# Last layer, second half of the batch: tile order by column pairs, and six of eight pairs turned by VectorE instead of TensorE

## The chip, the cores and the metric

The kernel runs on one core of a Trainium2 chip. The metric is the device time of one execution in microseconds; of the kernel before, three runs were timed, and the median is what is compared.

## What is computed

The reference takes x of shape (1024, 16, 16, 16): 1024 images of 16 rows (h), 16 columns (w) and 16 channels (c), float32. Four layers follow, each `x = x + layer(group_norm(x))`:

- layer 0, a tensor-train matrix on the 4096 values of an image;
- layer 1, a "cellular automaton" update: two fixed 3x3 depthwise filters, a dense layer 48 to 128 with relu, a dense layer 128 to 16, and a mask (alive or not, from a 3x3 maximum);
- layer 2, a 3x3 convolution;
- layer 3, the same kind of update as layer 1 with its own weights.

```
h = relu(flat @ fc0_w.T + fc0_b)
d = (h @ fc1_w.T + fc1_b).reshape(B, C, W, Hh)
xn = (xt + d) * (pre & post)
```

The result goes out in the layout of the input: batch, h, w, c.

## The kernel before, in words

**Tiling.** The batch is cut into two chunks of 512 images. Inside the layers the 512 images are the columns of a tile and 128 values of an image are its partitions; a chunk is 32 such tiles of 128x512 float32 (256 KB each). In layer 3 a tile is named by (q, w2): four channels (4q to 4q+3), two neighbouring columns (2·w2 and 2·w2+1, the "column pair" w2) and all 16 rows. The result wants images on partitions, so every tile of layer 3 has to be turned (transposed).

**The last stage.** The change is in the last stage, layer 3 on the second chunk, `layer_nca(X1, 1, 3, L3, xo)`, which takes the end of the span. Its work is driven by an order written out by `plan()`: a list of slots. A slot is either one matmul on each of up to four row groups of TensorE (tile `ph`, line L1466) or the second dense layer of one column of a tile (`fc1`, tile `po`, L1317). The result of a `ph` row is taken by ScalarE (relu into `hid`, L1469). A tile (q, w2) has two columns v = 0, 1, one "quad" m each, so there are 64 quads. Step by step:

- When a quad m begins, SyncE's DMA queue (SP) gets the load of the weights `wq` of quad m+2 (L1275, only for q > 0, five buffers), and, for the few columns that need them, four small copies `nx` (L1291) for a later quad: FAR quads ahead.
- At `fc1` of v = 0 SP gets the load of the residual tile `r` (L1298, four buffers).
- At `fc1` of v = 1 VectorE (DVE) makes `u` from `po` (L1329), which also frees the PSUM bank of `po` (two banks in all, shared with the turning); GpSimd (POOL) multiplies by the mask and adds to `r` (L1368, L1369). For q = 0 the masks come first (L1361, L1362).
- Eight slots later `turn` (L1378) transposes the four 128x128 blocks of `r` on TensorE into a PSUM bank `ptx`, and DVE copies it out (`evac`, L159, two copies per tile) into `xo`, which lies in the 8 MB of X0, free by then.

**Beside it.** The same stage brings the first chunk's result out: `output_steps(0)`, sixteen rounds h = 0..15. Each loads 512 KB of the finished first chunk from DRAM in four DMAs of 128 KB (`xs`, L963), turns it by four DVE block transposes (`xo`, L969) and stores 512 KB to the result (L974). `run()` spreads these steps over the stage: a step has a cost, its position is the sum of the costs ahead of it, and a step of cost 0 stands at the position reached so far, just ahead of the next step that has a cost. A `turn` of a round costs 1, its load and store cost 0. Two buffers `xs` and two `xo` are there, and the load of round h+1 is put ahead of the turn of round h.

**Queues.** Each engine works through its instructions in the order in which the program gives them, SP too: where an SP entry waits (for a buffer to be free, for data to be finished), the SP entries behind it wait with it. In the last stage SP's own waits show 79.8 us in 30 waits of a `wq` load (L1275) for TensorE.

**After the stage** eight DMAs of 1 MB (L1606) write the second chunk's result from X0.

Of the kernel before, what the change touches and what calls it, by code (L numbers as in the profile page):

```python
# [18 lines left out]
B, S, C = 1024, 16, 16  # L19
P = 128  # L20
NB = 512
# [82 lines left out]
def conv_preact_kernel(ctx: ExitStack, tc: tile.TileContext, a: dict, out: bass.AP):  # L104
    nc = tc.nc
    V, A, G, T = nc.vector, nc.scalar, nc.gpsimd, nc.tensor
# [9 lines left out]
    xf = [  # L116
        [dram.tile([8, 4, P, NB], F32, tag=f"xf{l}_{n}", name=f"xf{l}_{n}") for n in range(NCH)]
        for l in range(5)
    ]
# [7 lines left out]
    def stage(es, sb, ps):  # L127

        for key, sizes, kw in (("sb", sb, {}), ("ps", ps, {"space": PSUM})):
            p = es.enter_context(  # L130
                tc.tile_pool(name=f"{key}{len(pool)}", bufs=1, reuse_waits="tile", **kw)
            )
            pool[key] = p, sizes
        pool[len(pool)] = None

    def work(shape, tag, name, dt=F32):
        p, sizes = pool["sb"]
        return p.tile(shape, dt, tag=tag, name=name, bufs=sizes[tag])
# [10 lines left out]
    def psum(shape, name):  # L149
        return bank(shape, shared[0], name)  # L150
# [3 lines left out]
    def evac(dst, src):  # L154
        flip[0] ^= 1
        if flip[0] and not on_vector[0]:
            A.copy(dst, src)
        else:
            V.tensor_copy(dst, src)  # L159


    ident = const.tile([P, P], F32, tag="ident", name="ident")
# [504 lines left out]
    def rstd(st, rows=slice(0, P)):  # L667


        def root():  # L670
            st["t"] = work([P, NB], "s", "t")
            A.activation(st["t"][rows], st["ve"][rows], AF.Sqrt)

        def newton():
            ve, t = st["ve"][rows], st["t"][rows]
            st["r"] = work([P, NB], "n", "r")
            r = st["r"][rows]
            V.reciprocal(r, t)
            V.tensor_tensor(t, r, r, ALU.mult)
            V.tensor_tensor(t, t, ve, ALU.mult)  # L680
            V.tensor_scalar(t, t, -0.5, 1.5, ALU.mult, ALU.add)
            V.tensor_tensor(r, r, t, ALU.mult)

        return [2, root, 3, (6, newton)]
# [64 lines left out]
    def alone(N, q):  # L749

        return (
            N["sums"][q] + [3, N["mean"][q], 1, N["held"][q], 1] + N["sq"][q]
            + [3, N["var"][q], 1, N["keep"][q]]
        )
# [18 lines left out]
    def scaled(N, qs):  # L773
        steps = [N["spread"][qs[0]], 2, N["held"][qs[0]], 2]
        for q in qs:
            mul = N["mul"][q]
            if q < qs[-1]:
                mul = woven(mul, (2, N["spread"][q + 1]), (3, N["held"][q + 1]))
            steps += mul
        return steps  # L780
# [18 lines left out]
    def tile_cw(t, i):  # L799

        return t[i % 8, i // 8]
# [150 lines left out]
    def output_steps(n):  # L952

        steps = []

        lines = xf[4][n].rearrange("w q (c v h) b -> h (q c v) w b", v=2, h=S)

        def load(h, st):  # L960
            st["x"] = work([P, 8, P], "xs", "xs")
            for g in range(4):
                nc.sync.dma_start(st["x"][32 * g : 32 * g + 32], lines[h][:, :, P * g : P * g + P])  # L963

        def turn(h, st):
            st["o"] = work([P, 4, S, S], "xo", "xo")
            x = st["x"].rearrange("p w (j f) -> p f w j", f=4)
            for f in range(4):
                V.transpose(  # L969
                    st["o"][:, f].rearrange("p (w v) c -> p w c v", v=2), x[:, f]  # L970
                )

        def store(h, st):
            nc.sync.dma_start(  # L974
                out[n * NB : n * NB + NB, h].rearrange("(p f) w c -> p f (w c)", f=4),
                st["o"].rearrange("p f w c -> p f (w c)"),
            )

        sts = [{} for _ in range(S)]
        steps += [lambda: load(0, sts[0]), 4]  # L980
        for h in range(S):
            if h + 1 < S:
                steps.append((0, lambda h=h: load(h + 1, sts[h + 1])))
            steps += [lambda h=h: turn(h, sts[h]), (0, lambda h=h: store(h, sts[h]))]
        return steps


# [268 lines left out]
    def layer_nca(X, n, l, L, xo=None):  # L1256


        st = {}
        quads = [(q, w2, v) for q in range(4) for w2 in range(8) for v in range(2)]  # L1260
        AHEAD, FAR = 2, 3
        BANKS, SKEW = 6, (0, 1, 2, 1)

        def rows_of(q, w2, v):
# [99 lines left out]
        def residual(q, w2):  # L1364
            u, r = st["u", q, w2], st["r", q, w2]

            by = V if (q, w2) == (3, 7) else G
            by.tensor_tensor(u, u, st["m"][:, w2], ALU.mult)  # L1368
            by.tensor_tensor(r, r, u, ALU.add)  # L1369
            if xo is None:  # L1370
                after(7, lambda: nc.sync.dma_start(tile_cw(xf[l + 1][n], 8 * q + w2), r))
            else:
                after(8, lambda: turn(q, w2, r))

        def turn(q, w2, r):
            pt = psum([P, 4, 4, 2, S], "ptx")
            for bg in range(4):
                T.transpose(  # L1378
                    pt[:, bg].rearrange("p c v h -> p (c v h)"), r[:, bg * P : bg * P + P], ident
                )  # L1380
            for v in range(2):

                evac(
                    xo[:, :, :, 2 * w2 + v, 4 * q : 4 * q + 4].rearrange("p g h c -> p g c h"),
                    pt[:, :, :, v],
                )
# [7 lines left out]
        def after(n, fn):  # L1394
            later.append((st["slot"] + n, fn))
# [83 lines left out]
    def run(layer, us, loads, *spans, by=0.0):  # L1479

        start, main = layer
        start()
        loads, done = list(loads), 0
        todo = []
        for bg, lo, hi in spans:
            bg = [b if isinstance(b, tuple) else (1, b) if callable(b) else (b, None) for b in bg]
            idle = sum(b[0] for b in bg if b[1] is None) / (us * (hi - lo))  # L1490
            less = min(1.0, 0.7 / idle) if idle else 1.0
            weight = sum(b[0] for b in bg if b[1] is not None)
            at = lo
            for cost, step in bg:
                if step is None:
                    at += cost * less / us
                else:
                    todo.append((at, step))
                    at += (hi - lo) * (1 - idle * less) * cost / weight
        todo.sort(key=lambda x: x[0])  # L1500
        for i, step in enumerate(main):
            step()
            part = (i + 1) / len(main)
            while done < len(loads) and done < len(loads) * part / (by or 1e-9):
                loads[done]()
                done += 1
            while todo and (todo[0][0] < part or i == len(main) - 1):
                todo.pop(0)[1]()
# [4 lines left out]
    X0, X1 = XN  # L1513
# [18 lines left out]
    with ExitStack() as es:  # L1532
# [30 lines left out]
        for q in range(4):  # L1563
            bg = alone(N, q - 1) if q else [0.0]
            if q == 3:
                bg = bg + rstd(nst, slice(0, 96)) + [3] + scaled(N, range(3))
# [6 lines left out]
    nca_sb = dict(t4=2, s=3, n=2, wq=5, mask=1, f=5, hid=8, u=2, r=4, nx=1)  # L1573
    nca_ps = dict(h=6, o=2)
    conv_sb, conv_ps = dict(gn, s=3, r=12, hx=3), dict(o=6, m=2)
    on_vector[0] = True
    with ExitStack() as es:
        shared[0] = "o"
        stage(es, nca_sb, nca_ps)
        run(  # L1580
            layer_nca(X0, 0, 1, L1), 250, load_cw(X1, xf[1][1]), (last, 0.0, 0.18),
            (norm_cw(X1, False), 0.21, 1.0), by=0.3,
        )
        run(
            layer_nca(X1, 1, 1, L1), 245, load_wc(X0, xf[2][0]), (norm_lines(X0, False), 0.2, 1.0), by=0.3
        )
# [7 lines left out]
    with ExitStack() as es:  # L1594
        shared[0] = "o"
        stage(es, nca_sb, nca_ps)
        run(layer_nca(X0, 0, 3, L3), 245, load_cw(X1, xf[3][1]), (norm_cw(X1, False), 0.2, 1.0), by=0.3)
    with ExitStack() as es:
        stage(es, dict(nca_sb, xs=2, xo=2), nca_ps)

        xo = X0.rearrange("p n b -> p (n b)").rearrange("p (g h w c) -> p g h w c", g=4, h=S, w=S)
        run(layer_nca(X1, 1, 3, L3, xo), 280, (), (output_steps(0), 0.0, 1.0))
        for h in range(0, S, 8):
            for g in range(4):
                b0 = NB + g * P
                nc.sync.dma_start(  # L1606
                    out[b0 : b0 + P, h : h + 8].rearrange("b h w c -> b (h w c)"),
                    xo[:, g, h : h + 8].rearrange("p h w c -> p (h w c)"),
                )


# [25 lines left out]
```

## Time and profile before

| what | us |
|---|---|
| median of three runs (3052.56 to 3057.89) | 3057.21 |
| the profiled execution | 3054.15 |
| its span, first to last instruction | 3052.4 |
| last stage, first to last work on TensorE | about 2763 to 3030 |
| writing the second chunk's result out at the end | 3030 to 3052.4 |

In the profile PE is TensorE, PEld its weight loads, DVE VectorE, ACT ScalarE, POOL GpSimd, SP SyncE with its DMA queue. Lines such as L1378 are lines of the kernel before. A row of a group of instructions gives the line, engine, operation, output and input, how many, then busy time and the mean of one in ns, then idle time ahead of them and what ended it. The chain of waits follows the work that ended last backwards; the timeline gives start and duration of each instruction.

### The profile page before, as it was taken

Reading aid. Unit: us, or ns where it says so; the run is one execution under the profiler, and the core shown is the slowest. Engines: PE = TensorE matmul, PEld = TensorE weight load, DVE = VectorE, ACT = ScalarE, POOL = GpSimd, SP = SyncE. Lnnn points to the kernel's source line nnn. Section 1 sums busy time; section 2 is a strip of 40 time slices with the busy share of each in tenths; the row PEclk is TensorE's granted clock in tenths of the full one; section 3 lists DMA queues with packets and bytes.
Section 4 is the critical chain, followed back from the end, with each engine's and each line's share of the span. In section 5 each row is a group of like instructions: output and inputs, shape, how many; then the busy total and the mean of one; then the engine's idle time right before and its main releaser. Section 6 shows DMA issues by size and latency. Waiting matters only on the chain.

```text
span 3052.4 us, 36639 instructions
## 1 busy us (share of the span) xinstructions
PE 2982.6 (98%) x13746; PEld 1252.2 (41%) x13746; DVE 1757.4 (58%) x2338; ACT 1100.0 (36%) x1798; POOL 674.8 (22%) x732
## 2 busy tenths in 40 slices
PE   7999999999999999999999999999999999999996
PEld 5544334444444444444444433333333333333332
DVE  5254336555554555544555768756977766856432
ACT  4431341100000000000111156666667656666563
POOL 1114671200000000000000015434542223442331
PEclk8999999999999999999999999999999999999998
DMA  7642664533333433332222235436337866343555
GB/s 260 257 146 88 137 140 156 179 107 116 109 110 126 151 109 109 109 102 88 88 88 94 71 123 172 132 123 202 123 125 177 193 101 204 123 129 112 149 163 197
DMA packets 251809, 418.67 MB, mean 137 GB/s; under 512 B 35044, under 2 KB 105320, under 8 KB 248560
## 3 DMA queue, kind: packets, MB, share of 16 engines
q1 hardware_dynamic: 225376, 362.45, 35.9%
q0 software_dynamic: 25440, 53.58, 8.5%
q8 instruction: 109, 1.79, 0.2%
q14 instruction: 68, 0.56, 0.1%
q10 hardware_dynamic: 816, 0.30, 0.0%
HBM read 238.79 MB, written 165.60 MB: 132 GB/s over the span
## 4 chain that ended last, share of the span: by engine, by line
issue 47%; PE 43%; POOL 5%; DMA 1%; DVE 1%; ACT 0%; SPq 0%; POOLq 0%; DVEq 0%
PE ph L1466 17%; PE po L1098 13%; PE po L1317 6%; PE po L1193 2%; POOL u L1368 2%; POOL res L1369 2%; PE pw L1021 1%; PE L_conv_pe L392 1%; PE ptin L840 1%; POOL xf L1242 1%; PE ptx L1378 1%; DMA gq<-g_dram 0%; PE pr L739 0%; PE pvar L727 0%; PE pmean L723 0%
## 5 line engine op out<-in xcount | busy, mean ns | idle before, releaser
L1098 PE MATMUL po<-xn,w 128*128 128x512 f32 x3584 | 1577.4, 597 | 4.6 <-DVE xn L911 4.6
L1098 PEld LDWEIGHTS po<-xn,w 128*128 128x128 f32 x3584 | 672.3, 191 | 841.5 <-issue 818.3
L1469 ACT ACTIVATE hid<-ph,pack 128x512 f32<-128x512 f32 x1024 | 652.5, 686 | 380.5 <-PE ph L1466 271.0
L1134 DVE TENSOR_TENSOR r<-r,po 128x512 f32<-128x512 f32 x576 | 378.1, 684 | 577.0 <-PE po L1098 525.9
L1368 POOL TENSOR_TENSOR u<-u,mask 128x512 f32<-128x512 f32 x124 | 195.8, 1579 | 1817.4 <-DMA nx<-xn 1239.7
L1026 ACT COPY w<-pw 128x512 f32<-128x512 f32 (+1 forms) x320 | 150.6, 557 | 1214.4 <-issue 1014.5
L1466 PE MATMUL ph<-xn,wq 32*128 32x512 f32 x3664 | 565.7, 610 | 0.0
L1466 PEld LDWEIGHTS ph<-xn,wq 32*128 32x128 f32 x3664 | 232.8, 184 | 270.2 <-issue 238.2
L1466 PE MATMUL ph<-xn,pack 32*128 32x512 f32 x1288 | 297.5, 623 | 1.2 <-DVE mask L1362 0.9
L1317 PE MATMUL po<-hid,pack 128*32 128x512 f32 x2048 | 282.5, 606 | 2.7 <-ACT hid L1469 2.7
L1039 DVE TENSOR_TENSOR w<-w 128x512 f32<-128x512 f32 x320 | 210.5, 685 | 99.8 <-ACT w L1026 99.8
L640 DVE TENSOR_TENSOR xn<-xn,m 128x1024 f32<-128x1024 f32 x160 | 225.5, 1458 | 47.1 <-ACT m L655 47.0
L1329 DVE SCALAR_TENSOR_TENSOR u<-po,pack,xn 128x512 f32<-128x512 f32 x128 | 95.9, 749 | 204.7 <-PE po L1317 200.3
L1369 POOL TENSOR_TENSOR res<-res,u 128x512 f32<-128x512 f32 x124 | 207.5, 1673 | 9.7
L1193 PE MATMUL po<-xn,convw 128*128 128x512 f32 x368 | 166.8, 606 | 5.1 <-ACT conv L1241 5.1
L1466 PEld LDWEIGHTS ph<-xn,pack 32*128 32x128 f32 x1288 | 115.8, 185 | 98.4 <-issue 62.7
L1134 DVE TENSOR_TENSOR xn<-xn,po 128x512 f32<-128x512 f32 x96 | 64.4, 685 | 125.9 <-PE po L1098 125.8
L1317 PEld LDWEIGHTS po<-hid,pack 128*32 128x32 f32 x2048 | 43.1, 109 | 197.4 <-issue 137.7
L607 DVE TENSOR_TENSOR sq<-sq 128x1024 f32<-128x1024 f32 x78 | 106.9, 1370 | 13.1 <-ACT sq L625 10.8
L1193 PEld LDWEIGHTS po<-xn,convw 128*128 128x128 f32 x368 | 69.2, 193 | 102.1 <-issue 92.0
L404 POOL DMA_DIRECT2D L_conv_wy<-xn x160 | 88.8, 563 | 28.5 <-ACT xn L398 17.6
L1021 PE MATMUL pw<-R,gq 32*128 32x256 f32 (+1 forms) x1280 | 88.9, 383 | 2.3 <-DMA gq<-g_dram 2.3
(165 smaller groups left out, 1775.2 us busy)
## 6 DMA issues: line engine op xcount, KB each, us to landing
xf<-r SPq DMA_DIRECT2D x112, 512.0 KB, 3.9
xn<-xf SPq DMA_DIRECT2D x96, 512.0 KB, 5.0
r<-xf SPq DMA_DIRECT2D x80, 512.0 KB, 4.4
wq<-L_conv_wy SPq DMA_DIRECT2D x192, 192.0 KB, 2.7
res<-xf SPq DMA_DIRECT2D x128, 256.0 KB, 3.0
xf<-res SPq DMA_DIRECT2D x96, 256.0 KB, 2.0
res<-xr SPq DMA_DIRECT2D x256, 64.0 KB, 2.8
xf<-conv POOLq DMA_DIRECT2D x64, 256.0 KB, 6.0
```

Of the source, the lines that this page charges most:

```text
L640: V.tensor_tensor(part, part, m().unsqueeze(1).broadcast_to([P, 2, NB]), op)
L1021: T.matmul(pw[r][:, v], st["g", u][rows, v], st["R"][rows, p % 2, 64 * k0 : 256], start=True, stop=True,)
L1026: A.copy(w[:, k0:4, :, 32 * r : 32 * r + 32].rearrange("p k t (v o) -> p v (k t) o", v=2), pw[r],)
L1039: V.tensor_tensor(w[:, k], w[:, x], w[:, y], ALU.add if sign > 0 else ALU.subtract)
L1098: T.matmul(po, st["w", u][:, matrix, t], x, start=t == 0, stop=t == 3)
L1134: V.tensor_tensor(r[at], r[at], po, ALU.add if sign > 0 else ALU.subtract)
L1193: T.matmul(st["po", h][wh], conv["fw"][:, y], X[:, 16 * wh + h + y - 1], start=y == max(0, 1 - h), stop=y == min(2, S - h),)
L1317: T.matmul(po[32 * j : 32 * j + 32], nca["w1"][:, v], hid[j], start=v == 0, stop=v == 1)
L1368: by.tensor_tensor(u, u, st["m"][:, w2], ALU.mult)
L1369: by.tensor_tensor(r, r, u, ALU.add)
L1466: T.matmul(ph, w, x, start=k == 0, stop=k == len(tiles) - 1)
L1469: A.activation(h, ph, AF.Relu, bias=nca["bt"][:, r : r + 1])
```

## The change

In the last stage only:

1. The tiles of q = 1, 2, 3 are taken pair by pair (w2 outer, q inner) instead of q by q. The eight tiles of q = 0 stay first.
2. For the pairs w2 = 0 to 5 no tile is turned on TensorE. Each finished tile is stored to DRAM as in the other layers (seven slots after its residual step). When the tile of q = 3 of a pair is done, the pair is loaded back in two halves k = 0, 1 (`bring`, four DMAs of 128 KB each, 16 and 26 slots later) into the one buffer `xt`, and each half is turned by four DVE block transposes (`turn_blocks`, 25 and 35 slots later). Pairs 6 and 7 are turned on TensorE as before.
3. To make room there is one buffer `xs` and one `xo` instead of two each, and so the load of round h+1 of the first chunk's output comes after the turn and store of round h in the list of steps, not ahead of the turn of round h. `nx` has two buffers instead of one, and its copies are issued two quads ahead instead of three.
4. Images lie on partitions in another order in `xo` (image 4p+f on partition p, part f), so the last eight DMAs write rows of 8 KB that are four images apart.

```diff
@@ output_steps
         for h in range(S):
+            steps += [lambda h=h: turn(h, sts[h]), (0, lambda h=h: store(h, sts[h]))]
             if h + 1 < S:
                 steps.append((0, lambda h=h: load(h + 1, sts[h + 1])))
-            steps += [lambda h=h: turn(h, sts[h]), (0, lambda h=h: store(h, sts[h]))]
@@ layer_nca
-        quads = [(q, w2, v) for q in range(4) for w2 in range(8) for v in range(2)]
-        AHEAD, FAR = 2, 3
+        tiles_in_order = [(q, w2) for q in range(4) for w2 in range(8)]
+        if xo is not None:
+            tiles_in_order = tiles_in_order[:8] + [(q, w2) for w2 in range(8) for q in (1, 2, 3)]
+        quads = [(q, w2, v) for q, w2 in tiles_in_order for v in range(2)]
+        AHEAD, FAR = 2, 3 if xo is None else 2
+        BLOCKS = 6
...
-            if xo is None:
-                after(7, lambda: nc.sync.dma_start(tile_cw(xf[l + 1][n], 8 * q + w2), r))
-            else:
+            if xo is not None and w2 >= BLOCKS:
                 after(8, lambda: turn(q, w2, r))
+                return
+            after(7, lambda: nc.sync.dma_start(tile_cw(xf[l + 1][n], 8 * q + w2), r))
+            if xo is not None and q == 3:
+                for k in range(2):
+                    after(16 + 10 * k, lambda k=k: bring(w2, k))
+                    after(25 + 10 * k, lambda k=k: turn_blocks(w2, k))
+
+        def bring(w2, k):
+            x = st["xs", w2, k] = work([P, 8, P], "xt", "xt")
+            src = xf[l + 1][n][w2].rearrange("q (c v h) b -> (q c v) h b", v=2, h=S)
+            for g in range(4):
+                nc.sync.dma_start(
+                    x[32 * g : 32 * g + 32], src[:, 8 * k : 8 * k + 8, P * g : P * g + P]
+                )
+
+        def turn_blocks(w2, k):
+            x = st["xs", w2, k].rearrange("p h (j f) -> p f h j", f=4)
+            for f in range(4):
+                V.transpose(
+                    xo[:, f, 8 * k : 8 * k + 8, 2 * w2 : 2 * w2 + 2].rearrange("p h v c -> p h c v"),
+                    x[:, f],
+                )
@@ the stage
-        stage(es, dict(nca_sb, xs=2, xo=2), nca_ps)
+        stage(es, dict(nca_sb, nx=2, xs=1, xt=1, xo=1), nca_ps)
```

More of the change, by code (lines that the diff above doesn't have):

```diff
@@ L1369, in residual @@
             by.tensor_tensor(r, r, u, ALU.add)
-            if xo is None:
-                after(7, lambda: nc.sync.dma_start(tile_cw(xf[l + 1][n], 8 * q + w2), r))
-            else:
+            if xo is not None and w2 >= BLOCKS:
                 after(8, lambda: turn(q, w2, r))
+                return
[18 more added lines that the diff above has]
+                )
         def turn(q, w2, r):
             pt = psum([P, 4, 4, 2, S], "ptx")
-            for bg in range(4):
+            for f in range(4):
                 T.transpose(
-                    pt[:, bg].rearrange("p c v h -> p (c v h)"), r[:, bg * P : bg * P + P], ident
+                    pt[:, f].rearrange("p c v h -> p (c v h)"),
+                    r.rearrange("p (j f) -> p f j", f=4)[:, f], ident,
                 )
@@ L1598, in conv_preact_kernel @@
     with ExitStack() as es:
-        stage(es, dict(nca_sb, xs=2, xo=2), nca_ps)
-        xo = X0.rearrange("p n b -> p (n b)").rearrange("p (g h w c) -> p g h w c", g=4, h=S, w=S)
+        stage(es, dict(nca_sb, nx=2, xs=1, xt=1, xo=1), nca_ps)
+        xo = X0.rearrange("p n b -> p (n b)").rearrange("p (f h w c) -> p f h w c", f=4, h=S, w=S)
         run(layer_nca(X1, 1, 3, L3, xo), 280, (), (output_steps(0), 0.0, 1.0))
         for h in range(0, S, 8):
-            for g in range(4):
-                b0 = NB + g * P
+            for f in range(4):
                 nc.sync.dma_start(
-                    out[b0 : b0 + P, h : h + 8].rearrange("b h w c -> b (h w c)"),
-                    xo[:, g, h : h + 8].rearrange("p h w c -> p (h w c)"),
+                    out[NB : 2 * NB, h : h + 8].rearrange("(p f) h w c -> f p (h w c)", f=4)[f],
+                    xo[:, f, h : h + 8].rearrange("p h w c -> p (h w c)"),
                 )
```

## The prediction, made before the changed kernel ran

> **What bounds the kernel now.** First the page's head, to see which engine fills the span.
>
> ```profile
> span 3052.4 us, 36639 instructions
> PE 2982.6 (98%) x13746; PEld 1252.2 (41%) x13746; DVE 1757.4 (58%) x2338; ACT 1100.0 (36%) x1798; POOL 674.8 (22%) x732
> ```
>
> TensorE does. The change lies in the last stage alone, so second the table of windows for it (us, then busy time of PE, PEld, DVE, ACT, POOL, clock, DMA share, GB/s).
>
> ```profile
> 2763.00:3030.00 267.00, 262.54 (x2009) 100.22 (x2008) 115.73 (x199) 163.88 (x256) 75.42 (x62) 1.00 0.51 142
> 3030.00:3052.40 22.40, 0.00 (x0) 0.00 (x0) 0.06 (x1) 0.00 (x0) 0.00 (x0) 0.50 0.90 375
> ```
>
> TensorE is busy 262.5 of 267 us; DVE 43%, POOL 28%, DMA half. Then 22.4 us of output, which wait for the last turning. Third, the groups of the stage, shapes apart, for what is removed and added.
>
> ```profile
> L969 DVE STREAM_TRANSPOSE xo<-xs 128x256 f32<-128x256 f32 x64 | 36.6, 660 | 0.0
> L159 DVE COPY xn<-ptx 128x256 f32<-128x256 f32 x64 | 33.4, 603 | 33.4 <-PE ptx L1378 33.4
> L1378 PE MATMUL ptx<-ident,res 128*128 128x128 f32 x128 | 20.9, 286 | 3.1 <-DVE res L1369 1.9 <-DVE xn L159 1.2
> ```
>
> DVE never sits idle ahead of L969 (0.0): the output rounds of the first chunk find their data there. Fourth, the chain of waits, for what one turning is worth in TensorE's time.
>
> ```profile
> 2995.04 0.59 PE ptx L1378 x4
> 2995.63 2.79 PE ph L1466 x24
> 2998.41 1.00 PE po L1317 x8
> ```
>
> One turned tile: 0.59 us. 24 records of ph are three slots, 0.93 us each; an fc1 slot is 1.00. Fifth, SP's timeline, because the change reorders and adds DMAs, and DVE's beside it for the turns.
>
> ```profile
> 2862.01 0.60 SPq L974 DMA_DIRECT2D out_dram<-xo  x1
> 2862.66 3.08 SPq L963 DMA_DIRECT2D xs<-xf  x4
> 2865.84 4.74 SPq L1275 DMA_DIRECT2D wq<-L_conv_wy  x2
> ...
> 2876.35 0.55 SPq L974 DMA_DIRECT2D out_dram<-xo  x1
> 2876.95 3.02 SPq L963 DMA_DIRECT2D xs<-xf  x4
> ```
>
> ```profile
> 2866.16 2.30 DVE L969 STREAM_TRANSPOSE xo<-xs 128x256 f32<-128x256 f32 x4
> 2883.26 2.26 DVE L969 STREAM_TRANSPOSE xo<-xs 128x256 f32<-128x256 f32 x4
> ```
>
> ```profile
> xs<-xf SPq DMA_DIRECT2D x44, 128.0 KB, 4.5
> ```
>
> The load issued at 2862.66 is turned at 2883.26: it has a whole round (17 us) of lead. But SP passes that place only 4.2 us ahead of DVE's next turn (2862.01 against 2866.16). Over the nine rounds from 2862 to 2988 this distance is 4.2, 6.9, 8.8, -0.4, 0.8, 4.0, 7.7, 1.2 and -7.1 us, 2.9 in the mean.
>
> [...] L1378 needs the copies of L159 behind it, L969 none. [...] copies, u and turns of DVE follow program order. [...] a load of stored data has to wait for the store's completion; SP's waits show one such, 1.6 us, L963 for xf<-res. [...] The trace shows 0.50 only in the idle tail, no gap inside a stage.
>
> **The change, part by part.**
>
> TensorE: 24 of 32 tiles are no longer turned there, 24 x 0.59 = 14.2 us. The new order makes the planner's list 238 slots instead of 241 (174 ph slots with work instead of 176): 2 x 0.93 = 1.9. Gain 16.1 us, all on the path, since TensorE is the bound.
>
> DVE, amount: away 48 copies x 0.603 = 28.9 us, new 48 transposes (4 x 2 x 6, of L969's shape) x 0.66 = 31.7. Plus 2.8 us on an engine at 43%: nothing by itself. Banks: without ptx between them, `po` has a bank free for a tile longer; worth at most the 3.0 us that PEld waits for L159, taken as nothing.
>
> SP and DMA, amount: 24 stores x 0.40 (0.32 and its gap, stage before this one) and 48 loads x 0.72 (L963, 2.9 per four): 44 us more to issue. Bytes 6.3 MB out and 6.3 back, 12.6 on 142 GB/s x 267 us = 37.9 MB: a share of about 0.68, no bound.
>
> The reorder of the output rounds, where I see the cost. A step of cost 0 stands directly ahead of the next step that has one. In the new list store(h) and load(h+1) both fall directly ahead of turn(h+1), and nothing is loaded a round earlier. From SP's arrival there, store 0.65 + four loads 2.9 + landing 4.5 = 8.05 us pass until DVE can turn; SP arrived 2.9 us ahead on average. DVE waits the rest, with everything behind it in line: the u of the tile (and `po`'s bank), the turn_blocks, the last copies. For the u waits POOL's residual, for that SP's store of the tile, and behind that store stand bring, `wq` and the next load. So the round is a ring DVE, POOL, SP, DMA. Prices: landing 4.5, turn 2.3 (four back to back), u 0.8, POOL to the end of its add 2.6 (1.16 + 1.28 and gaps), turn_blocks 2.3, store of a tile 0.4, bring 2.9, wq or residual load 0.5, four nx 2.8, output store 0.65, xs 2.9. TensorE needs 14 slots per round (10.5 x 0.93 + 3.5 x 1.00 = 13.3 us; 13 slots, 12.4, in round 8).
>
> - Round 9 to 10: landing 4.5, turn 2.3, u 0.8, turn_blocks 2.3, then SP: bring 2.9, residual, wq, store, wq 1.9, nx 2.8, output store 0.65, xs 2.9: 21.05, 7.75 too long.
> - Round 8 to 9: 4.5 + 2.3 + 0.8 + 2.6 + 0.4 + bring 2.9 + 0.5 + 0.65 + 2.9 = 17.55, 5.15 too long.
> - The others the same way, by what stands in each queue between the loads: 4 to 5 1.35, 5 to 6 2.55 (SP's own work, 15.85), 6 to 7 0.85, 7 to 8 5.25, 10 to 11 6.95, 11 to 12 5.45, 12 to 13 4.35, 13 to 14 3.05, 14 to 15 5.1.
>
> Sum 47.8 us by which turn(15) comes late. TensorE has cover: two banks let u be some 10 us late, wq is asked for two quads (7.6 us) ahead. But cover is used once, and at the end it is short: the copies of tile (3,6) stand behind turn(15) and hold a bank that the turning of (1,7) needs 8 slots (7.6 us) later, after 2.3 + 1.05 of DVE's work: 4.2 us of slack, about what DVE is late at turn(4) already (8.05 - 2.9 = 5.1). So TensorE loses about 48 us. If the landing counts from the start of an issue, each round is 0.7 shorter: 40. I take 44. Net 44 - 16 = 28 us.
>
> Other unknowns: pair order lets each `nx` be used every other quad, with two buffers; four copies are 2.8 us on SP, in the rounds above. Clock after gaps [...] taken 0, because it waits for the ring anyway. Landing times under 33% more bytes: from 0 to +1 us a round, 0 to 11; taken 0. The output at the end: same bytes, rows further apart, -1 to +2; taken 0.
>
> **Sum.** Profiled execution 3054.15 (span 3052.4 and 1.75 around it) + 28 = 3082; it lies 3.06 below the median, so 3057.2 + 28 = 3085.
>
> **Rivals.**
> - SP comes early (ends faster). Nothing but the full buffers held SP back before (79.8 us in 30 waits of L1275 for PE ph); if it reaches the output store 8 us ahead of each turn, or the rings come to 13.3 us, TensorE never waits and the 16 us show: 3041. For it: DVE is idle half the time. Against: 44 us more issue, and stores that wait for POOL. It needs each ring 4.3 us (47.8/11) shorter; that is the point from which it decides.
> - The ring costs as much as the turning gives: 1.5 us a round, 16 in all: 3057.
> - The ring with slower landings (1 us a round)[...].
>
> **Chances.** Ring 0.63 (3068 to 3100), SP early 0.16, even 0.09 (same 0.06, faster 0.02, slower 0.01), ring with congestion 0.12 (3100 to 3115). Faster by over 0.2%: 0.18; within 0.2%, about what a measurement of this kernel can tell from no change, 0.06; slower 0.76. Leaving out the early SP (0.16) and 0.04 above: 3049 to 3112.
>
> **What would show it.** Right: DVE idle ahead of the output turns (0.0 us before), ended by DMA xs, several us in most rounds from 7 on; TensorE's waits for wq, nx and for DVE's u or copies; the stage some 295 us instead of 267, with PE's busy time near 247. Waits for POOL at SP's tile stores. Wrong: output turns without a wait, xs landing a round ahead, TensorE busy throughout and the stage 251 us. Partly wrong: DVE waits, but TensorE doesn't, because the banks cover it.

## The result and the profile after

| | before | after |
|---|---|---|
| median of four runs each (us) | 3057.55 (3052.56 to 3058.11) | 3079.12 (3075.38 to 3082.09) |
| profiled execution (us) | 3054.15 | 3076.46 |
| its span (us) | 3052.4 | 3074.5 |
| last stage: from the start of the last `po` group of the stage before it to the last work on TensorE (us) | 267.7 | 290.2 |
| from there to the end of the span (us) | 23.4 | 23.4 |

The ratio of the times is 1.0072, 95% interval 1.006 to 1.0084: slower by 21.6 us. The stage alone accounts for it (22.5 us); the output at the end takes what it took. Where the stage starts differs by up to 10 us between the executions profiled for this document (2757.5 to 2767.3 us), though nothing ahead of it was changed, and so the length of the stage itself is given beside the times below.

The page's head, after:

```profile
span 3074.5 us, 36547 instructions
PE 2983.9 (97%) x13650; PEld 1244.6 (40%) x13650; DVE 1759.5 (57%) x2338; ACT 1100.5 (36%) x1798; POOL 676.0 (22%) x732
```

TensorE's busy time is 1.3 us higher than before although 24 tiles are no longer turned there, and the span is 22 us longer. The windows of the last stage say why (us, busy time of PE, PEld, DVE, ACT, POOL, then clock, DMA share, GB/s):

```profile
2763.00:2830.00 67.00, 66.38 (x478) 23.79 (x475) 34.57 (x55) 45.78 (x72) 14.59 (x12) 1.00 0.48 141
2830.00:2890.00 60.00, 58.58 (x455) 22.17 (x454) 22.04 (x38) 35.76 (x59) 21.87 (x18) 1.00 0.74 208
2890.00:2950.00 60.00, 55.87 (x404) 18.47 (x402) 18.56 (x33) 33.19 (x51) 14.59 (x12) 0.94 0.74 201
2950.00:3010.00 60.00, 48.27 (x365) 17.20 (x359) 23.10 (x41) 30.01 (x46) 14.82 (x13) 0.91 0.69 185
3010.00:3054.00 44.00, 34.42 (x225) 12.68 (x223) 18.50 (x34) 18.83 (x29) 9.55 (x8) 0.87 0.48 136
```

In the first 67 us, the tiles of q = 0, TensorE is busy throughout, as before. From 2890 on TensorE is idle for 4 and 12 us in 60, and its clock, 1.00 in each of these windows up to 3010 before, falls to 0.94, 0.91 and 0.87. DMA is busy for three quarters at most. Now the groups of the stage:

```profile
L969 DVE STREAM_TRANSPOSE xo<-xs 128x256 f32<-128x256 f32 x64 | 36.3, 648 | 106.2 <-DMA xs<-xf 92.9 <-DMA wq<-L_conv_wy 7.9 <-DMA nx<-xn 5.4
L1396 DVE STREAM_TRANSPOSE xn<-xt 128x256 f32<-128x256 f32 x48 | 27.4, 655 | 4.0 <-DMA xt<-xf 4.0
L1404 PE MATMUL ptx<-ident,res 128*128 128x128 f32 x32 | 6.7, 339 | 8.1 <-DVE xn L159 5.7 <-DVE res L1374 1.4 <-POOL res L1374 1.0
```

DVE's idle time ahead of the output turns is 106.2 us, where it was 0.0; the new block turns cost what the old shape costs (655 ns) and wait for hardly anything. TensorE's own waits in the stage, and SP's (total, times, longest):

```profile
PE ph L1493 <- DMA wq<-L_conv_wy: 15.5, 7, 6.3
PE ptx L1404 <- DVE xn L159: 5.7, 2, 4.5
```

```profile
SPq L1378 <- POOL res L1374: 54.2, 13, 12.7
SPq L1389 <- DVE xn L1396: 35.0, 7, 7.9
SPq L1280 <- PE ph L1493: 17.9, 14, 3.5
```

TensorE's matmuls wait for weights, which they never did in this stage before. SP, which before was held by TensorE (79.8 us in 30 waits for a free `wq` buffer), is now held mostly by POOL at the tile stores and by DVE at bring. One round shows how the two meet. DVE's timeline (start, us; in brackets the idle time before):

```profile
2948.68 2.25 DVE L969 STREAM_TRANSPOSE xo<-xs 128x256 f32<-128x256 f32 x4 [12.30 <-DMA xs<-xf]
2950.82 2.26 DVE L1396 STREAM_TRANSPOSE xn<-xt 128x256 f32<-128x256 f32 x4
2952.97 0.72 DVE L1334 SCALAR_TENSOR_TENSOR u<-po,pack,xn 128x512 f32<-128x512 f32 x1
2967.42 2.24 DVE L969 STREAM_TRANSPOSE xo<-xs 128x256 f32<-128x256 f32 x4 [13.72 <-DMA xs<-xf]
```

SP's timeline over the same round:

```profile
2942.68 2.75 SPq L963 DMA_DIRECT2D xs<-xf  x4
2945.47 0.45 SPq L1303 DMA_DIRECT2D res<-xf  x1
2946.02 0.38 SPq L1280 DMA_DIRECT2D wq<-L_conv_wy  x1
2946.49 0.38 SPq L1378 DMA_DIRECT2D xf<-res  x1
2953.11 1.80 SPq L1389 DMA_DIRECT2D xt<-xf  x4
2955.01 0.39 SPq L1280 DMA_DIRECT2D wq<-L_conv_wy  x1
2955.45 2.41 SPq L1296 DMA_DIRECT2D nx<-xn  x4
2957.91 0.58 SPq L1303 DMA_DIRECT2D res<-xf  x1
2958.59 0.40 SPq L1280 DMA_DIRECT2D wq<-L_conv_wy  x1
2959.09 0.38 SPq L1378 DMA_DIRECT2D xf<-res  x1
2959.52 0.61 SPq L974 DMA_DIRECT2D out_dram<-xo  x1
2960.18 3.28 SPq L963 DMA_DIRECT2D xs<-xf  x4
```

Read it as a circle. The xs load issued at 2942.68 has landed by 2948.68 (6.0 us). DVE, idle for 12.3 us until then, turns it, then makes the block turn that stands behind it, to 2953.08. SP is through with everything it may do at 2946.9 and stands at bring (2953.11), which needs the one `xt` that this block turn reads; behind bring are eight issues of other DMAs, the output store and the next xs load, at 2960.18. From load to load it takes 17.5 us; TensorE needs 13.3 for the same work, by the prediction's count of slots.

### The profile page after: what moved, and what is told of

It reads as the page before. It is cut to its first block, busy times and chain, and to the rows that moved or that the text cites. A ratio compares the mean times of both kernels' runs of the same rounds, so it can differ in the third digit from the quotient of the medians.

```text
span 3074.5 us, 36547 instructions
## 1 busy us (share of the span) xinstructions
PE 2983.9 (97%) x13650; PEld 1244.6 (40%) x13650; DVE 1759.5 (57%) x2338; ACT 1100.5 (36%) x1798; POOL 676.0 (22%) x732
## 4 chain that ended last, share of the span: by engine, by line
issue 47%; PE 41%; POOL 5%; DMA 2%; DVE 1%; SPq 1%; ACT 0%; POOLq 0%; DVEq 0%
PE ph L1493 15%; PE po L1098 13%; PE po L1322 6%; POOL u L1373 2%; POOL res L1374 2%; PE po L1193 2%; PE pw L1021 1%; PE L_conv_pe L392 1%; PE ptin L840 1%; POOL xf L1242 1%; DMA wq<-L_conv_wy 1%; SPq L963 0%; DMA gq<-g_dram 0%; PE pr L739 0%; PE pvar L727 0%
## 5 line engine op out<-in xcount | busy, mean ns | idle before, releaser
L1493 PE MATMUL ph<-xn,wq 32*128 32x512 f32 x3664 | 576.4, 617 | 15.8 <-DMA wq<-L_conv_wy 15.5
L969 DVE STREAM_TRANSPOSE xo<-xs 128x256 f32<-128x256 f32 x64 | 36.3, 648 | 106.2 <-DMA xs<-xf 92.9
L404 POOL DMA_DIRECT2D L_conv_wy<-xn x160 | 89.1, 564 | 29.4 <-ACT xn L398 15.5
```

What stands on the lines that cost most here:

```text
L1493: T.matmul(ph, w, x, start=k == 0, stop=k == len(tiles) - 1)
```

## The experiments

Each was timed against the kernel before on the same chip, so the ratios can be compared throughout, the medians only roughly: the kernel before read 3058.05, 3057.16, 3053.13 and 3059.43 beside E1 to E4, E5 to E8, E9 and E10, E11 and E12. Three more numbers are read from each trace, that is from one execution: the length of the last stage, taken as in the table above; DVE's idle time ahead of L969; and the time from the start of turn(4), the first with a wait of 5 us in the changed kernel, to the end of TensorE's work.

| kernel | median us | ratio to before (95%) | stage | DVE idle ahead of L969 | turn(4) to end |
|---|---|---|---|---|---|
| before | 3057.55 | 1 | 267.7 | 0.0 | 181.1 |
| after | 3079.12 | 1.0072 (1.006 to 1.0084) | 290.2 | 106.2 | 199.8 |
| E1 load early | 3048.52 | 0.9974 (0.9963 to 0.9984) | 259.9 | 6.2 | 175.7 |
| E2 list alone, in before | 3077.66 | 1.0064 (1.005 to 1.0077) | 289.8 | 59.7 | 189.2 |
| E3 E1, pairs on TensorE | 3058.65 | 1.0003 (0.9994 to 1.0012) | 269.3 | 2.3 | |
| E4 after without bring and block turns | 3047.09 | 0.9964 (0.995 to 0.9978) | 258.7 | 89.4 | 168.3 |
| E5 E1, rounds forward | 3047.66 | 0.9975 (0.9966 to 0.9984) | 259.0 | 6.7 | |
| E6 after without block turns | 3055.58 | 1.0001 (0.9992 to 1.001) | 266.1 | 100.0 | 175.9 |
| E7 after without bring | 3047.82 | 0.9971 (0.9961 to 0.9982) | 260.0 | 75.5 | 170.1 |
| E8 E1, xs loads from GpSimd | 3049.60 | 0.9974 (0.9963 to 0.9985) | 257.3 | 13.6 | |
| E9 after, bring from GpSimd | 3065.85 | 1.0033 (1.002 to 1.0046) | 275.6 | 55.6 | 185.8 |
| E10 after, tile stores from GpSimd | 3081.94 | 1.0092 (1.0075 to 1.0109) | 292.2 | 109.7 | 201.6 |
| E11 after, two xt, seven hid | 3069.59 | 1.0029 (1.0018 to 1.0041) | 279.3 | 82.6 | 182.5 |
| E12 after, seven hid | 3087.89 | 1.0095 (1.0078 to 1.0113) | 299.0 | 101.6 | 202.4 |

The theory was that of the prediction: the load of round h+1, now directly ahead of its turn, closes a ring through the queues of DVE and SP. Against it stood the 44 us of added issue on SP wherever the load stands, and the pair order.

**E1, the load earlier.**

```diff
-            steps += [lambda h=h: turn(h, sts[h]), (0, lambda h=h: store(h, sts[h]))]
+            steps += [(0.2, lambda h=h: turn(h, sts[h])), (0, lambda h=h: store(h, sts[h]))]
...
+            steps.append((0.8, lambda: None))
```

> The changed kernel with one thing moved: store(h) and load(h+1) of the first chunk's output stand a fifth of a round (some 3 of 14 slots) behind turn(h) instead of directly ahead of turn(h+1); same buffers, same number of DMAs. Theory (ring through the late load): DVE's idle time ahead of L969 falls from 106 us to under 20, TensorE's waits in the stage nearly vanish, and the 16 us of saved turning show: 3041 us (3037 to 3050). Rival A (SP and the DMA engines have simply too much to do, 72 more DMAs): the order of the list changes little, 3065 to 3080. Rival B (the pair order itself starves TensorE of nx and wq): as slow as the changed kernel, 3070 or more.

3048.52 us, 30.6 below the changed kernel with all its work and the same buffers (30.3 in the stage). A group, SP's wait at bring and TensorE's wait for weights in E1:

```profile
L969 DVE STREAM_TRANSPOSE xo<-xs 128x256 f32<-128x256 f32 x64 | 36.4, 648 | 6.2 <-DMA xs<-xf 6.2
```

```profile
SPq L1390 <- DVE xn L1397: 18.6, 5, 4.5
PE ph L1494 <- DMA wq<-L_conv_wy: 5.6, 3, 3.0
```

Position alone undoes the loss (the output store moves with the load): the same number of DMAs, issued by the same engine, costs nothing visible in DVE's idle time when the load stands most of a round ahead. The rival of SP's amount falls. Bring still waits 18.6 us for DVE's block turns, but the xs load is then already out, so the wait closes no circle. E1 stays 7.5 us over the 3041 that were expected.

**E2, the new list in the kernel before.** The order of the steps from the changed kernel, and one `xs` and one `xo`; everything else as before.

```diff
+            steps += [lambda h=h: turn(h, sts[h]), (0, lambda h=h: store(h, sts[h]))]
             if h + 1 < S:
                 steps.append((0, lambda h=h: load(h + 1, sts[h + 1])))
-            steps += [lambda h=h: turn(h, sts[h]), (0, lambda h=h: store(h, sts[h]))]
...
-        stage(es, dict(nca_sb, xs=2, xo=2), nca_ps)
+        stage(es, dict(nca_sb, xs=1, xo=1), nca_ps)
```

> The kernel before with only the new list of the output steps and one buffer xs and one xo; tiles in the old order, all turned on TensorE, no tile stored and brought back. Theory (the ring needs the tile stores that make SP wait for POOL, and the brings): DVE waits ahead of L969, 40 to 60 us in all, but SP isn't held by POOL, so the waits don't add up from round to round; TensorE, whose PSUM bank is covered by some 4 us only, loses 3 to 18 us: 3066 us. Rival A (amount of DMA work): no more DMAs than before, so 3057. Rival C (the late load alone is the whole cost, ring or not): 44 us lost, 3095 or more.

3077.66: the late load costs 19.6 us here (22.1 in the stage), twice what was expected, with no bring and no stores of these tiles. TensorE's waits in E2:

```profile
PE po L1317 <- DVE u L1329: 10.1, 4, 7.3
PE po L1317 <- DVE xn L159: 7.1, 1, 7.1
```

They aren't for weights but for a PSUM bank: in the old order the copies out of `ptx` and the `u` of a tile stand behind the waiting L969 in DVE's queue, and `ptx` shares the two banks with `po`. So a late load has two ways to TensorE: by the weights in the new order, by the banks in the old one.

**E3, E1 with all pairs turned on TensorE** (`BLOCKS = 0` in place of 6), for the value of the block turns and of the pair order.

> As e1, but no pair goes by DRAM: all 32 tiles are turned on TensorE, in the pair order, with the load early. Theory: only the pair order is left, two slots of the planner's list fewer, 1.9 us: 3055 us (3051 to 3060); against e1 it shows what the turning on DVE is worth, 14 us. Rival B (pair order starves TensorE): 3065 or more. Rival A: about 3056, as there are no brings.

3058.65, the time of the kernel before within its interval: the pair order with one `xs` and the load in good time costs nothing, and that rival falls. Against E1 the turning of 24 tiles on TensorE costs 10.1 us (9.4 in the stage), not 14.2. The turning itself is dearer here than before:

```profile
L1405 PE MATMUL ptx<-ident,res 128*128 128x128 f32 x128 | 23.9, 309 | 3.0 <-DVE res L1375 1.8 <-DVE xn L159 1.2
```

309 ns of one against 286 before, 3.0 us in all, with the clock at 1.00 in both; what differs in these matmuls is that they read every fourth column of `res`.

**E4, the changed kernel without bring and without block turns.**

```diff
             if xo is not None and q == 3:
-                for k in range(2):
-                    after(16 + 10 * k, lambda k=k: bring(w2, k))
-                    after(25 + 10 * k, lambda k=k: turn_blocks(w2, k))
+                pass
```

> The changed kernel without bring and turn_blocks: pairs 0 to 5 of the second chunk are stored to DRAM but not brought back and turned, so these columns are missing in the result. The late load stays. Theory (ring): bring (2.9 us) and turn_blocks (2.3 us) drop out of rounds 7 to 15, the rounds come to about 13 us, DVE still waits ahead of L969 (some 50 us), but TensorE hardly: 3046 us (3041 to 3055). Rival C (the late load alone is the cost): 3070 or more. Rival A: also fast, so this run separates the ring from C only.

3047.09, the size that was expected. But in E4 SP still waits for POOL, and DVE still for xs:

```profile
SPq L1378 <- POOL res L1374: 71.0, 15, 12.7
```

```profile
L969 DVE STREAM_TRANSPOSE xo<-xs 128x256 f32<-128x256 f32 x64 | 36.6, 655 | 89.4 <-DMA xs<-xf 74.6 <-DMA wq<-L_conv_wy 9.4 <-DMA nx<-xn 5.5
```

89.4 us of idle DVE and 71.0 us of SP's waits for POOL cost next to nothing: from round 7 to 15 the turns come every 13.7 us (17.4 in the changed kernel), near the 13.3 that TensorE needs. Idle time ahead of L969 is therefore no measure of the loss. That the banks and the weights asked for early cover it as long as it doesn't grow from round to round is how we read this; no run tests the cover alone.

**E5, E1 with the early rounds shorter** (0.65 of a round's cost for h below 8, 1.35 from 8 on), to move output rounds away from the part with brings.

> As e1 (load early), with the output rounds of the first chunk spaced unevenly: rounds 0 to 7 get 0.65 of an even share of the stage, rounds 8 to 15 1.35, so that fewer of them fall beside the brings. What e1 still loses is two gaps of TensorE of 5 us in all, ended by wq loads that stood in SP's queue behind output loads, nx copies and a bring. If that is so, these gaps close: 3044 us (3039 to 3049), 4 to 5 us under e1. If SP's amount of work limits e1, not the collision of groups, nothing is gained: 3048.

3047.66, not to be told from E1. A window and TensorE's wait for weights in E5:

```profile
2920.00:2950.00 30.00, 28.72 (x220) 9.77 (x216) 9.78 (x17) 17.11 (x26) 7.44 (x7) 0.94 0.75 203
PE ph L1495 <- DMA wq<-L_conv_wy: 2.1, 2, 1.3
```

The waits for `wq` fell from 5.6 to 2.1 us and the time did not follow (the stage is 0.9 us shorter); these waits alone are not the 7 us to the expected 3041. The clock is at 0.94 in the window shown, though no wait was longer than 1.3 us.

**E6, without the block turns alone, and E7, without bring alone.** E6 leaves out the two lines `after(25 + 10 * k, ... turn_blocks ...)`; E7 leaves out the lines `after(16 + 10 * k, ... bring ...)` and lets the block turns read X1 in SBUF.

> The changed kernel with its late load and with the brings on SP, without turn_blocks on DVE: the six pairs are loaded back but not turned, so these columns are missing in the result. It splits what e4 took away. The ring's rounds without turn_blocks (2.3 us, and SP's wait for them) are 1 to 6 us shorter from round 9 on: about half of the changed kernel's loss is left, 3056 us (3049 to 3066). If the brings' time on SP alone makes the loss, 3075 or more; if turn_blocks on DVE does, 3048, as e4.

> The other half: late load, no brings; turn_blocks turns data that lies in SBUF already (the stage's own input), so the six pairs are wrong in the result. The rounds lose bring's 2.9 us and SP's wait for DVE: some 15 to 17 us by the prediction's prices, less by what these were too high; the banks' cover takes most of it: 3051 us (3046 to 3060). If turn_blocks on DVE alone makes the loss, 3070 or more.

3055.58 and 3047.82. Against E4, by the medians, bring alone costs 8.5 us, the turns alone 0.7, and both together (the changed kernel) 32.0. The sum of the parts is 9, so 23 us belong to their meeting. The stages give the same (7.4, 1.3 and 31.5, hence 22.8); the ratios give some 20 (11, 2 and 33). Two waits are there only when both are there: bring's for the block turn of the half before, in the one `xt` (35.0 us in the changed kernel), and the block turn's for the data of bring (4.0 us). The first was the new theory, and the next runs were chosen for it.

**E8, E1 with the xs loads issued from GpSimd's queue** (`G.dma_start` in L963).

> As e1, with the 64 xs loads issued from POOL's queue instead of SP's: SP has 64 issues (46 us) less, its wq and brings never stand behind an output load. If SP's queue is what e1 still loses to: 3044 us. POOL waits in its own order for the turn of round h and issues, which delays a tile's residual by some 3 us, covered. If POOL's issues are dear or their landing slow (6 us in the page for POOL's conv stores against 4.5), DVE waits ahead of L969 again: 3050 to 3060.

3049.60, no difference from E1 by the medians (the stage is 2.6 us shorter): once the load is early, SP's order is not, or not much of, what keeps the time above 3041.

**E9, the changed kernel with bring issued from GpSimd** (`G.dma_start` in place of `nc.sync.dma_start` in bring).

> The changed kernel, with the 48 loads of bring issued from GpSimd's queue instead of SP's; nothing else moves and all the work is done. Theory (each round is a ring that closes through SP's own order, in which bring's 1.8 to 3.3 us of issue stand between DVE's last turn and the next xs load): the ring gets 1.8 to 3.3 us shorter in eight rounds, most of the 22 us loss goes: 3055 to 3062, DVE idle ahead of L969 below 80 us. Rival (it is the data, not the place in SP's order: 12.6 MB more in flight, landings of xs and wq longer): 3076 to 3082, since all transfers are still made at about the same times. Second rival (GpSimd, held by bring's wait for the stores, makes the residuals late and the ring closes there): 3070 to 3080, with GpSimd's queue waiting for xs or for the stores.

3065.85, above the range of the theory and below those of both rivals. POOL's waits and DVE's in E9:

```profile
POOL xt L1389 <- DVE xn L1396: 21.1, 5, 6.0
```

```profile
L969 DVE STREAM_TRANSPOSE xo<-xs 128x256 f32<-128x256 f32 x64 | 36.3, 646 | 55.6 <-DMA xs<-xf 34.4 <-DMA nx<-xn 18.0 <-DMA wq<-L_conv_wy 2.8
L1396 DVE STREAM_TRANSPOSE xn<-xt 128x256 f32<-128x256 f32 x48 | 27.2, 643 | 45.0 <-DMA xt<-xf 45.0
```

```profile
SPq L1378 <- POOL res L1374: 87.2, 16, 13.4
```

SP is free of the wait, and DVE idles half as long ahead of the output turns; but it now waits 45.0 us for the data of bring ahead of the block turns (4.0 in the changed kernel). The wait stands in POOL's queue, ahead of the residuals that SP's stores wait for (87.2 us against 54.2). Bandwidth was not what was short here (the DMA share is 0.74 to 0.78 from 2830 to 3010 and 0.69 to 0.74 in the changed kernel). E9 moves a wait to another queue besides the issue time; which of the two brings the 13 us isn't separated.

**E10, the changed kernel with the tile stores of the last stage from GpSimd**, behind its own residual.

> The changed kernel, with the tile stores of the last stage issued from GpSimd's queue, directly behind its own residual work; SP no longer waits for GpSimd there (54 us in 13 waits in the changed kernel). All the work is done. Theory (the ring runs DVE, POOL, SP, DMA, and the store's wait for POOL is a link of it): SP reaches the xs load earlier in the rounds whose link it is, a half to all of the 22 us goes: 3055 to 3066. Rival (SP's wait for POOL is slack, the link is bring's wait for DVE's turn of the half before, L1389 <- xn, 35 us in 7 waits): 3074 to 3082, the wait moves to bring.

3081.94: nothing won, as the rival had it. SP's waits in E10:

```profile
SPq L1390 <- DVE xn L1397: 51.2, 8, 8.7
SPq L1303 <- DMA xf<-res: 38.8, 7, 9.2
```

The 54.2 us of waits for POOL are gone and have gone to bring (35.0 before, 51.2 now) and to the residual loads, whose buffer the store must have left first. So SP's wait for POOL was slack in front of others; but as the stores, and with them the residual loads, still depend on POOL, this run alone doesn't clear POOL. E4 and E7 do so better: there SP waits for POOL for 71.0 and 80.5 us, and nothing is lost.

**E11, two buffers `xt`**, paid for with one of eight `hid`, and **E12**, that payment alone.

```diff
-        stage(es, dict(nca_sb, nx=2, xs=1, xt=1, xo=1), nca_ps)
+        stage(es, dict(nca_sb, nx=2, xs=1, xt=2, xo=1, hid=7), nca_ps)
```

> The changed kernel with two buffers xt instead of one, so that a bring no longer waits for the block turn of the half before it; paid for with seven hid buffers instead of eight. Theory (this wait, 35 us in 7 on SP, is the link by which DVE's lateness gets back to the next xs load): SP passes bring without waiting, the ring is cut, 3056 to 3066. Rival (either link alone closes the ring: the wait moves to the tile stores, L1378 for POOL, 54 us before): 3072 to 3082.

> The changed kernel with seven hid buffers instead of eight and nothing else, the control of the run with two xt: 3078 to 3086 if the eighth buffer matters little, as expected, since ScalarE is at 36%.

E12 reads 3087.89, dearer than expected: the missing `hid` costs some 7 to 9 us (7.0 by the ratios, 8.8 by the medians and by the stage), and most of it lies ahead of turn(4), since from there to the end it takes 202.4 us against 199.8. E11 against its control is 18.3 us faster (19.7 in the stage), from turn(4) on 19.9. SP's waits in E11, with no line for bring's wait for DVE any more, and TensorE's:

```profile
SPq L1378 <- POOL res L1374: 74.4, 16, 13.1
SPq L1280 <- PE ph L1493: 23.7, 19, 4.5
```

```profile
PE ph L1493 <- DMA wq<-L_conv_wy: 7.7, 7, 2.0
```

POOL holds SP for longer than in the changed kernel (74.4 us against 54.2), and TensorE waits half as long for weights (7.7 us; 15.5 in the changed kernel, 14.8 in E12). The rival, that the wait would move to the tile stores and cost the same there, falls: the link that costs most is bring's wait for the one `xt`. Some 11 us of the 30 by which the changed kernel's stage is longer than E1's remain in E11 (30.3 - 19.7, if the missing `hid` costs the same in E11 and E12), near the 9 that bring and the turns cost with a late load when they don't meet. And the clock, E11's windows:

```profile
2890.00:2950.00 60.00, 57.20 (x446) 21.14 (x445) 22.84 (x40) 37.09 (x56) 17.54 (x15) 1.00 0.83 218
2950.00:3010.00 60.00, 53.39 (x418) 19.46 (x414) 24.57 (x43) 33.79 (x52) 15.05 (x13) 1.00 0.85 232
```

With seven waits for weights of at most 2.0 us it stays at 1.00; with seven of up to 6.3 us it was 0.94 and 0.91. More bytes pass in the same time (218 and 232 GB/s against 201 and 185), so the transfers didn't limit the changed kernel.

## Why the prediction was right, and where its steps were off

Predicted 3085, measured 3079.12, in the direction forecast and by the cause that was named, the late load. That the sum came so near is in part luck, as two of its terms were too large and cancelled in part. The pieces fare as follows.

**The circle of waits: right, one link wrong.** Most of the named signs came: DVE idle ahead of L969 (106.2 us, most of it from round 7 on), TensorE's waits for `wq` and for the copies, SP's waits for POOL, and a stage of 290 us, where 295 were named. Waits of TensorE for `nx` or for `u` did not come, nor did a busy time near 247 us (see the clock below). E1 shows the cause. But the prediction closed the ring over "DVE, POOL, SP, DMA", the tile's store being the link. E4, E7 and E11 show that SP's wait for POOL is not what costs: it is longer in all three than in the changed kernel, and the time is shorter. The ring that costs most goes from DVE straight to SP, by bring's wait for the `xt` that the last block turn still reads (E11: 18 of the 30 us). The prediction's round 9 to 10 has that path, with bring's issue behind turn_blocks, but it didn't name the buffer, and its general ring goes by POOL. It also didn't have the way of E2, where a late load costs 19.6 us by the banks with no second stream at all.

**The rounds.** From turn to turn, predicted and measured:

| round | predicted | measured |
|---|---|---|
| 4 to 5, 5 to 6, 6 to 7 | 14.65, 15.85, 14.15 | 14.82, 16.24, 14.38 |
| 7 to 8, 8 to 9 | 18.55, 17.55 | 17.42, 16.46 |
| 9 to 10, 10 to 11 | 21.05, 20.25 | 18.06, 18.74 |
| 11 to 12, 12 to 13 | 18.75, 17.65 | 17.84, 18.79 |
| 13 to 14, 14 to 15 | 16.35, 18.4 | 15.20, 17.00 |
| all | 193.2 | 184.95 |

The excess over TensorE's pace (145.4 us for the eleven rounds) is 39.5 us instead of 47.8. Two prices were too high: four loads of bring issue in 1.80 us where SP has been standing before them, not 2.9, and the data are there some 3 to 4 us after the last issue of the four (3.3 and 4.0 in the xs loads of the round shown), not 4.5. From SP's arrival at the output store to the turn, 8.05 us by the prediction, the round shown takes 7.90 (2959.52 to 2967.42).

**TensorE's loss: 44 predicted, 30.6 measured** (after against E1). In the stages of these two traces the difference is 30.3: TensorE's listed waits are 15.4 us longer (24.2 against 8.8), and 9.5 is work at a lower clock (below); some 5 us stay open. The rest of the turns' lateness didn't reach TensorE; we put this down to the banks and to the weights asked for early, as E4 with its 89 us of idle DVE suggests.

**TensorE's gain: 16.1 predicted, 8 to 11 measured** (E1 and E4 against before: 9.5 and 11.0 by the medians, 7.8 and 9.0 by the stages; 10.1 for the block turns in E1 against E3). This term was too large by a third or more. The traces show four small things that the prediction didn't take off:

| us | E1 | E4 | E5 | E8 |
|---|---|---|---|---|
| TensorE's waits for `wq` | 5.6 | 2.7 | 2.1 | 2.5 |
| work lost to the lower clock | 1.7 | 1.7 | 1.7 | 0.0 |
| strided transposes of eight tiles (a quarter of E3's 3.0) | 0.8 | 0.8 | 0.8 | 0.8 |
| eleven or twelve quads of 3.96 us where the usual ones take 3.79 | 1.9 | 2.0 | 1.9 | 1.9 |
| 16.1 less these | 6.1 | 8.9 | 9.6 | 10.9 |
| stage shorter than before by | 7.8 | 9.0 | 8.7 | 10.4 |

This is an estimate added up from the traces, not an experiment on each part; it comes within 2 us in all four. The longer quads stand right behind the tiles of q = 0, and the trace of before has none; in E1 six of the eleven read no `nx`, so these copies don't explain them, and what does stays open.

Both terms of the sum, loss and gain, were too large, by 13 and by some 6, so that the errors partly cancel: 28 predicted, 21.6 measured.

**The clock: taken as 0, and it wasn't.** The prediction expected PE's busy time in the stage near 247 us; it is 263.5. E1, with the same work, has 246.9 in the same windows, and 1.8 us of work more ahead of them: 14.8 us of difference. In windows of 1 us the clock in the changed kernel's stage is at 1.00 or at 0.50, or crosses between them. Busy time in each such window times what its clock is short of 1.00 gives an estimate of the work lost: 11.2 us in the changed kernel, 1.7 in E1, 10.9 in E12 and none in E11. So 9.5 of the 14.8 us are the clock, and the rest stays open. The same estimate puts over half of the 19.7 us between the stages of E11 and E12 down to the clock. How much of the 11.2 us would otherwise have been waiting for the ring isn't separated by any run; the prediction's reason for 0, that TensorE waits for the ring anyway, is therefore neither shown nor refuted.

The gaps of 6.3 and 4.5 us in the changed kernel have 10.2 us at 0.50 each, which begin in the gap. But shorter ones are followed by 0.50 as well: those of 1.8 and 2.3 us in the changed kernel by 3.4 us of it each, and behind one of 2.0 in E1, one of 1.8 in E4 and one of 1.3 in E5 the windows (0.97 over 60 us, 0.97 over 60, 0.94 over 30) give about as much. One of 1.9 in the changed kernel, one of 3.0 in E1 and one of 2.4 in E7 are not followed by it (1.00 in E1's and E7's windows of 60 us). The length of the gap alone therefore doesn't decide here. The prediction's reading, 0.50 only in the idle tail, holds for the stage before but not for that whole trace: from 1794 to 1800 us TensorE works at 0.50, after a gap of 2.7 us.

**Nothing by amount: right.** DVE's 2.8 us don't show (E7: 0.7 us for the turns alone). With the load early, all of the added work costs nothing visible (E1's stage, with all of it, is within 1.2 us of that of E4, which has no bring and no block turns). With the load late, bring costs 7 to 11 us without its wait for DVE (E6 against E4). DMA at 0.69 to 0.74 of its time in the changed kernel was no bound: E5 reaches 1.00 in one window (2860 to 2890), with TensorE busy for all 30 us of it. The output at the end: 23.4 us in both.

## What to carry to other kernels

A load that moves behind the use of its buffer costs little while every wait downstream is covered (E4, 0.9964 of the kernel before), and a lot where it holds up something that TensorE soon needs (the banks in E2, 1.0064) or where the queues close a circle: here the late load holds DVE, DVE holds the one buffer of a second stream, and that stream's load stands ahead of the next load in SP's queue. Look for the circle and not for the longest wait: of SP's two the longer (54 us, for POOL) cost next to nothing and the shorter (35 us, for DVE) some 18 us. When buffers are given up to make room for a second stream, see first that each remaining load stands in good time (E1, 0.9974 of the kernel before); that did more here than a second buffer (E11).

## What the runs showed of the hardware that was not expected

- Turning 128x128 float32 blocks on TensorE took 286 ns each from 128 neighbouring columns and 309 ns from every fourth column (128 of each, before and E3, clock 1.00).
- Four 128-KB loads issued on SP in 1.80 to 3.28 us in the round shown, the shortest after a pause of SP. The weights of 192 KB landed 4.1 us after issue in the changed kernel from 2840 to 3050 us (median of 39).
- A gap of only 1.3 us in TensorE's work was followed by some 3.4 us at half clock (E5, at 2936; 0.94 over 2920 to 2950), which cost more work (1.7 us by the estimate above) than the gap itself; a gap of 3.0 us was not followed by it (E1, at 2958; 1.00 over 2950 to 3010). The two longest in the changed kernel, 6.3 and 4.5 us, had 10.2 us of it each.
- One `hid` buffer less of eight cost some 7 to 9 us (E12 against after), though ScalarE is busy for little over half of the stage (163.6 of 291 us in the changed kernel).
